# Cross-attention block with an MLP: gelus moved behind a copy, one normalization moved to VectorE, two batches' row loads moved into the fc pairs

## Chip, cores and metric

The kernel runs on one core of a Trainium2 chip. The metric is the device time of one execution in microseconds (us), lower is better; of several runs the median counts. The engines that matter here are TensorE (PE; PEld is its weight load), VectorE (DVE), ScalarE (ACT), GpSimd (POOL) and the queue of SyncE (SP), which issues most DMAs. Each engine works through its own list of instructions in order; semaphores tie the lists together.

## What is computed

Four batches (B = 4), 512 queries and 512 keys each, width 512, 16 heads of 32, inner width 2048, all in float32:

```python
residual = hidden
x = layer_norm(hidden, ln1_w, ln1_b)
q = (x @ q_w + q_b);  k = (ctx @ k_w + k_b);  v = (ctx @ v_w + v_b)      # split into heads
attn = softmax(where(mask, q k^T / sqrt(32), lowest))
hidden = (attn v) @ cproj_w + cproj_b + residual
y = layer_norm(hidden, ln2_w, ln2_b)
y = gelu(y @ fc_w + fc_b, approximate=True)
out = hidden + y @ proj_w + proj_b
```

## The kernel before

**Order.** Nothing is scheduled by a tool: the program order of each engine is the order in which the Python code emits instructions. The attention is emitted as 32 blocks (`block`), two for each of 16 groups `w` (a group is four heads of one batch; half a group is 256 queries). A table `fills` says for each block which other matmul work is put between its parts, to keep TensorE busy while VectorE and ScalarE work at the softmax: projections to q, k and v of later groups (`prep_q`, `prep_k`, `prep_v`), the output projection of a batch (`cproj`), transposes of normalized rows (`ln_turn`), and the MLP of batch 0 and half of batch 1. Each item has a cost (`CHAIN` = 3.4 for one accumulation chain, more for an fc pair); `run(work, budget)` emits items until the budget is used.

**A block.** `block` (L280) emits eight score tiles of [128, 512] (`scores`, L260), each into a PSUM bank of its own; there are eight banks, handed out in turn. `soften` adds the mask and takes the row minimum on VectorE (L266) and the exponential on ScalarE (L270). `turn` transposes 32x32 blocks on VectorE (L278). After the last exponential VectorE takes the reciprocal of the sums, and ScalarE spreads it (`rr`, L298, the "small copy"), VectorE transposes it (L301). `exchange` copies and DMAs the transposed weights between partitions, and a later `attend` multiplies them with v (L356) and divides (L361). ScalarE's tables hold either the exponential or the gelu: a switch is a table load in the trace.

**An fc pair.** The MLP's first matmul is done two f-chunks at a time by a Strassen-Winograd scheme of seven products (`fc_seven`, L487 on): product q1 goes to a bank, ScalarE copies it to `p1` (L518), and VectorE combines the other products with it in four additions (L471) that read the banks and write the pre-activation `g`. Then a gelu with the bias is due (L536), two activations for a pair. For pairs within the attention phase that gelu isn't emitted at once but put into a list, `S["gelu"]`, with the half `q` of the buffer that it works on; `gelus()` empties it. It is emptied in the next block directly behind the small copy `rr` (the call in `block`), inside `fc_seven` directly behind the copy to `p1`, and ahead of a projection that reads the half (`proj`, L571). In the pairs after the attention phase (`q is None`) the gelu is emitted directly.

**Normalization.** `ln_norm` (L143) computes (x - mean) * rstd for a tile of 128 rows, on ScalarE (L145) for the keys listed in `NORM_ACT`, otherwise on VectorE (L149). For `(2, 0)`, the second layer norm of batch 0, all four tiles are on ScalarE. `norm2(0, ...)` stands in the fill of block 10; the transposes to `yT` follow in the same block (L158), with their evictions on ScalarE (L163) and VectorE (L161).

**The last phase.** After the attention, `last_mlps` runs three MLPs: the other half of batch 1 (pairs 4 to 7), batch 2 and batch 3 (pairs 0 to 7 each). For each pair it emits weight sums for the next pair (`sum_wa`), the pair, the load of the weights of the pair after the next (`load_wa`, L595), in batch 1 also a load of projection weights (L814), and after every second pair the sums of two pairs' activations (`g_sums`, four operations on VectorE from SBUF to SBUF, L468 and L471). `project` then multiplies with the second weight matrix: a first product `q1p` (L716) that takes the last pair at the end, then `sums()`, then the other products (L698, or L661 where a second level of Strassen is used), the transposes of the next batch (`turns`), and the additions to the residual rows `hid` (`join`), whose results are stored.

**The residual rows.** The rows (attention result plus residual) of the later batches were written to a scratch tensor `xa` in HBM. `load_hid(b, ts)` reads them back by DMA on SP's queue (L412) and then adds the bias row `proj_b` on GpSimd (L367, one operation of [128, 512] for each of four tiles). In the trace the tile is `hl` for batch 2 and `hid` for the others. `sums()` in `last_mlps` calls it for the next batch, that is in the projection phase of the batch before:

```python
            def sums(b=b, new=new):
                for c in new[::2]:
                    p_sums(c)
                if b + 1 < B:
                    load_hid(b + 1, range(NT))
```

Of the kernel before, what the change touches and what calls it, by code (L numbers as in the profile page):

```python
# [21 lines left out]
B, L, D, H = 4, 512, 512, 16  # L22
HD = D // H
INNER = 4 * D
NT = L // P
# [8 lines left out]
SPLIT = 1  # L34
# [5 lines left out]
NORM_ACT = BY_ACT + ((2, 0), (2, 1))  # L40
# [10 lines left out]
def xattn_block(ctx: ExitStack, tc: tile.TileContext, x, encT, mask, q_w, k_w, v_w, c_w, fc_w, p_w, vecs, rows, out):  # L51
# [61 lines left out]
    S = {"gelu": []}  # L113
# [27 lines left out]
            S["nm", key] = nm  # L141

    def ln_norm(key, t, dst, src):  # L143
        if key in NORM_ACT:
            nc.scalar.activation(  # L145
                dst, src, AF.Identity, bias=S["nm", key][:, t : t + 1], scale=S["rs", key][:, t : t + 1]
            )
            return
        nc.vector.tensor_scalar(  # L149
            dst, src, S["mv", key][:, t, 0:1], S["rs", key][:, t : t + 1], ALU.subtract, ALU.mult  # L150
        )
# [103 lines left out]
    def scores(w, qt):  # L255
        qT, kT = S["qT", w], S["kT", w]
        S["sc", w, qt] = [acc_tile(f"sc_{w}_{qt}_{h}") for h in range(HG)]
        for h in range(HG):
            r = slice(h * HD, (h + 1) * HD)
            nc.tensor.matmul(S["sc", w, qt][h], qT[r, ts(qt, P)], kT[r, :], start=True, stop=True)  # L260

    def soften(w, qt, *heads):
        for h in heads:
            s = score_tile()
            mn = small.tile([P, 1], F32, tag="mn", bufs=2 * HG, name=f"mn_{w}_{qt}_{h}")
            nc.vector.tensor_tensor_reduce(  # L266
                out=s, in0=S["sc", w, qt][h], in1=S["mb", w // NG], scale=1.0, scalar=FMAX,
                op0=ALU.add, op1=ALU.min, accum_out=mn,
            )
            nc.scalar.activation(s, s, AF.Exp, bias=mn, scale=-1.0, accum_out=S["sums", w][:, qt, h : h + 1])  # L270
            if h % 2:
                S["ps", w, qt, h // 2] = score_pair()

    def turn(w, qt, k):

        tb = S["tb", w, qt // 2]
        tv = tb[:, :, :PW].rearrange("p j (a t h q) -> p a h t j q", a=2, t=NT, h=HG)
        nc.vector.transpose(tv[:, qt % 2, 2 * k : 2 * k + 2], S["ps", w, qt, k])  # L278

    def block(w, half, fill):  # L280

        q0, q1 = 2 * half, 2 * half + 1
        if half == 0:
            S["sums", w] = small.tile([P, NT, HG], F32, tag="sums", name=f"sums_{w}")
        tb = S["tb", w, half] = two.tile([P, NI, PW + 2 * HD], F32, tag="tb", name=f"tb_{w}_{half}")
        scores(w, q0)
        scores(w, q1)
        soften(w, q0, 0, 1, 2, 3)
        soften(w, q1, 0, 1)
        turn(w, q0, 0)  # L290
        turn(w, q0, 1)
        soften(w, q1, 2, 3)
        fill(0)
        turn(w, q1, 0)
        rs = small.tile([P, 2, HG], F32, tag="rsum", name=f"rsum_{w}_{half}")
        nc.vector.reciprocal(rs, S["sums", w][:, 2 * half : 2 * half + 2, :])
        rr = one.tile([P, 2, HG, HD], F32, tag="rr", name=f"rr_{w}_{half}")
        nc.scalar.copy(rr, rs[:, :, :, None].broadcast_to([P, 2, HG, HD]))  # L298
        gelus()
        turn(w, q1, 1)  # L300
        nc.vector.transpose(  # L301
            tb[:, :, PW:].rearrange("p j (a q) -> p a j q", a=2), rr.rearrange("p a h d -> p (a h d)")
        )
        waiting.append((w, half))
        last = w == NW - 1 and half
        if last:
            exchange()
        fill(1)
        if not last:
            exchange()  # L310
        fill(2)
# [7 lines left out]
    def exchange():  # L319

        while waiting and target(*waiting[0]) not in held:
            w, half = waiting.pop(0)
            held[target(w, half)] = w, half
            copies(w, half)
# [41 lines left out]
    def add_row(h, i):  # L366
        nc.gpsimd.tensor_tensor(h, h, row[:, i, :], ALU.add)  # L367
# [39 lines left out]
    def load_hid(b, ts_):  # L407

        for t in ts_:
            if ("hid", b, t) not in S:  # L410
                S["hid", b, t] = hids.tile([P, D], F32, tag="hid", name=f"hid_{b}_{t}")
            Q[0].dma_start(out=S["hid", b, t], in_=S["xa", b][ts(t, P), :])  # L412
        for t in ts_:
            add_row(S["hid", b, t], 1)

    def stat2(b, t):
        ln_stat((2, b), t, S["h", b, t])

    def norm2(b, t):
        h = S["h", b, t]  # L420
        y = tiles.tile([P, D], F32, tag="xn", name=f"xn2_{b}_{t}") if stays(b, t) else h
        S.setdefault(("yn", b), {})[t] = y
        ln_norm((2, b), t, y, h)
# [73 lines left out]
        return acc_tile(name).rearrange("p (i l) -> p i l", i=2)  # L497

    def gelus(q=None):
        while S["gelu"] and q in (None, S["gelu"][0][0]):  # L500
            S["gelu"].pop(0)[1]()

    def fc_seven(b, c, g, a, s, half, q=None):

# [34 lines left out]
        if q is None:  # L539
            gelus()  # L540
# [52 lines left out]
    def load_wa(c):  # L593
        for i in range(2):
            nc.sync.dma_start(out=wa[c % 2][:, i], in_=fc_w[:, 2 * c + i, :, :])  # L595

    def sum_wa(c):
        a = wa[c % 2]
        a_sums(a[:, 0, :2], a[:, 0, 2:], a[:, 1, :2], a[:, 1, 2:], *(ws[c % 2][:, i] for i in range(4)))
# [7 lines left out]
    def last_mlps():  # L607
# [71 lines left out]
        def g_sums(c):  # L679
            c = slice(c, c + 2)  # L680
            a11, a12, a21, a22 = (ga[:, c, k, j * HL : (j + 1) * HL] for j in range(2) for k in range(2))
            a_sums(a11, a12, a21, a22, gs[:, 0, c], gs[:, 1, c], a21, gs[:, 2, c])

        def fc_pair(b, c, sums):
            sums()
            fc_seven(b, c, ga[:, c], [wa[c % 2][:, i] for i in range(2)],
                     [ws[c % 2][:, i] for i in range(4)], half_tile)
# [97 lines left out]
        half = FIRST * FQ // 2  # L785
# [6 lines left out]
        def split(n):  # L792
            for _ in range(n):
                to_split.pop(0)()

        for b, pairs, new in (
            (SPLIT, range(half, NP), range(half)), (SPLIT + 1, range(NP), ()), (SPLIT + 2, range(NP), ())
        ):
            for c in pairs:

                def sums(b=b, c=c):
                    if c + 1 < NP:
                        sum_wa(c + 1)
                    split(splits.get((b, c), 0))

                fc_pair(b, c, sums)
                if c + 2 < NP:
                    load_wa(c + 2)
                elif b + 1 < B:
                    load_wa(c + 2 - NP)  # L810
                if new:
                    n = (c - half + 2) % half
                    for i in range(2):
                        nc.sync.dma_start(out=pb[:, n, i, :], in_=p_w[ts(2 * n + i, P), :])  # L814
                if c % 2 == 0 and c != pairs[0]:
                    g_sums(c - 2)

                if b == B - 3 and c < NP - 1:
                    stat2(B - 1, c - pairs[0])
                if b == B - 2:  # L820
                    if c == 0:
                        stat2(b + 1, NT - 1)
                        ln_rs((2, b + 1))
                    for t in {4: (0,), 5: (1, 2), 7: (3,)}.get(c, ()):
                        norm2(b + 1, t)
            g_sums(NP - 2)

            def sums(b=b, new=new):
                for c in new[::2]:
                    p_sums(c)  # L830
                if b + 1 < B:
                    load_hid(b + 1, range(NT))

            def turns(b=b):
                if b + 1 < B:
                    run(turns2(b + 1))
                if b == SPLIT:
                    load_xn(B - 1)

            def middle(b=b):  # L840
                if b + 1 < B:
                    y_sums(b + 1)
                    sum_wa(0)

            project(b, pairs, sums, turns, middle)
# [3 lines left out]
    CHAIN, TURN = 3.4, 0.5  # L849
# [115 lines left out]
    ahead, fills = {}, {}  # L965
# [20 lines left out]
    k, q, v = A(7)  # L986
    c, t2 = C(0), turns2(0)
# [4 lines left out]
    k, q, v = A(8)  # L992
    put(10, [k], norm(0, 0, 1), [v], norm(0, 2, 3), do(fc_sums), [q], t2, do(lambda: y_sums(0)))
    k, q, v = A(9)
# [4 lines left out]
    k, q, v = A(10)  # L999
# [4 lines left out]
    k, q, v = A(11)  # L1004
    put(16, h_(1, 0, 1), [k, q], x3[:2], some(2), x3[2:3])
    put(17, [v], x3[3:], h_(1, 2, 3), x4, cb(1), C(1))
    k, q, v = A(12)
    put(18, [q], some(2), [k])
    put(19, some(2), [v])
    k, q, v = A(13)  # L1010
    put(20, [k, q], stat(1, 0, 1, 2, 3), rs(1), some(2))
    put(21, [v], some(2))
    k, q, v = A(14)
# [3 lines left out]
    k, q, v = A(15)  # L1017
    c = C(2)
# [11 lines left out]
    for p in range(2 * NW):  # L1030
        w, half = divmod(p, 2)
        if half == 0 and w and w % NG == 0:
            make_mb(w // NG)
        run(ahead[p])
        for pair in due.get(p, ()):
            attend(*divmod(pair, 2))

        def fill(n, work=fills[p]):
            if n or not work or work[0][0] <= CHAIN:
                run(work, CHAIN if n < 2 else None)  # L1040

        block(w, half, fill)

    gelus()
    first_c = FIRST * FQ // 2
# [10 lines left out]
    c = C(B - 1)  # L1056
# [49 lines left out]
```

## Time and profile before

| | |
|---|---|
| median of three runs | 776.76 us (776.3 to 777.96) |
| the profiled execution's own time | 777.77 us |
| its span in the profile | 776.0 us |
| TensorE busy (matmul) | 770.2 us, 99% of the span |
| VectorE busy | 619.3 us, 80% |
| ScalarE busy | 337.3 us, 43% |
| GpSimd busy | 298.9 us, 39% |
| mean DMA rate | 154 GB/s |

How to read it: the span is what the hardware profiler saw of one execution; the rest of that execution's time, 1.77 us, lies around it. A matmul's end is modelled, so a matmul that stands a little longer in the record than its kind usually does has in most cases waited. In a timeline, the text in brackets at the end of a row is how long the engine was idle ahead of the instruction and what ended the wait. "x8" groups neighbouring instructions of one kind; a group's time runs from the first start to the last end, so a wait inside a group shows as a longer group. PEclk is the clock that TensorE was granted, 1.00 being full.

### The profile page before, as it was taken

The numbers are of one execution on the slowest core, as the hardware profiler recorded it, in microseconds if no ns is written. First come the engines' busy times: TensorE is split into PE (matmuls) and PEld (weight loads), VectorE is DVE, ScalarE is ACT, GpSimd is POOL, SyncE is SP. The second block draws the span as 40 slices with busy tenths as digits, with TensorE's granted clock in tenths as the row PEclk, the third lists the DMA queues.
The fourth block names the chain that finished last, engine by engine and source line by source line (L and its number), as shares of the span: only waits on it lengthen the run. The fifth ranks groups of instructions, "written<-read, shape, count | busy, mean of one in ns | idle before, by whom it ended". The sixth has DMA issues, their size and how long they took to land.

```text
span 776.0 us, 12991 instructions
## 1 busy us (share of the span) xinstructions
PE 770.2 (99%) x4450; PEld 522.3 (67%) x4450; DVE 619.3 (80%) x1262; ACT 337.3 (43%) x761; POOL 298.9 (39%) x311
## 2 busy tenths in 40 slices
PE   9999999999999999999999999999999999999998
PEld 7656455566654745565554566446888889988897
DVE  3889899886888757887888988856878999669863
ACT  2676766574675445737753467501201221012200
POOL 1525446378353264233575444430060024300052
PEclk9999999999999999999999999999999999999999
DMA  8978779456755666665657866683623330023001
GB/s 326 322 224 226 180 197 274 108 149 167 204 146 155 181 183 168 162 177 130 162 127 193 215 195 194 151 256 122 196 92 92 95 110 14 29 82 95 1 16 41
DMA packets 54817, 119.37 MB, mean 154 GB/s; under 512 B 10416, under 2 KB 13616, under 8 KB 54624
## 3 DMA queue, kind: packets, MB, share of 16 engines
q1 hardware_dynamic: 53712, 115.71, 53.5%
q0 software_dynamic: 896, 2.82, 1.2%
q8 instruction: 35, 0.57, 0.3%
q14 instruction: 30, 0.25, 0.1%
q10 hardware_dynamic: 144, 0.02, 0.0%
HBM read 58.22 MB, written 6.82 MB: 84 GB/s over the span
## 4 chain that ended last, share of the span: by engine, by line
PE 93%; DVE 4%; ACT 1%; issue 1%; POOL 0%; DVEq 0%; POOLq 0%
PE q L515 24%; PE accp L571 11%; PE sc L260 9%; PE av L356 7%; PE r L661 7%; PE accc L396 7%; PE accv L240 7%; PE acck L217 7%; PE accq L229 7%; PE q4p L698 2%; PE tp L158 2%; PE q1p L716 1%; DVE ptt L266 1%; DVE ga L471 1%; DVE gs L468 1%; PE warm L898 1%
## 5 line engine op out<-in xcount | busy, mean ns | idle before, releaser
L270 ACT ACTIVATE ptt<-ptt,mn 128x512 f32<-128x512 f32 x256 | 181.6, 711 | 157.2 <-DVE mn L266 157.2
L266 DVE CUSTOM_DVE_ANT_0 ptt<-sc,mb 128x512 f32<-128x512 f32 x256 | 160.5, 682 | 17.3 <-PE sc L260 17.3
L278 DVE STREAM_TRANSPOSE tb<-ptt 128x1024 f32<-128x1024 f32 x128 | 153.5, 1218 | 0.3 <-ACT ptt L270 0.2
L334 POOL COPY pT<-tb 32x1088 f32<-32x1088 f32 x96 | 104.3, 1086 | 42.6 <-DVE oT L361 20.9
L571 PE MATMUL accp<-pbt,gt 128*128 128x512 f32 x192 | 86.6, 606 | 0.0
L515 PE MATMUL q<-yT,gt 128*128 128x256 f32 x320 | 78.9, 379 | 0.0
L260 PE MATMUL sc<-pbt 32*128 32x512 f32 x512 | 71.3, 616 | 0.2 <-DVE gt L471 0.2
L571 PEld LDWEIGHTS accp<-pbt,gt 128*128 128x128 f32 x192 | 36.4, 193 | 47.0 <-issue 40.6
L536 ACT ACTIVATE ga<-ga,vec 128x512 f32<-128x512 f32 x40 | 26.7, 715 | 94.9 <-DVE ga L471 94.9
L515 PEld LDWEIGHTS q<-yT,gt 128*128 128x128 f32 x320 | 60.9, 190 | 8.6 <-issue 0.5
L240 PEld LDWEIGHTS accv<-ptt,xe 128*128 128x128 f32 x512 | 59.1, 192 | 7.4 <-DVE mn L266 4.7
L515 PE MATMUL q<-ys,gt 128*128 128x256 f32 x240 | 61.7, 380 | 0.0
L240 PE MATMUL accv<-ptt,xe 128*128 128x128 f32 x512 | 60.0, 276 | 0.0
L217 PE MATMUL acck<-xe,ptt 128*128 128x512 f32 x128 | 58.8, 602 | 0.0
L229 PE MATMUL accq<-xe,ptt 128*128 128x512 f32 (+1 forms) x136 | 58.3, 573 | 0.0
L396 PE MATMUL accc<-wc,oT 128*128 128x512 f32 x128 | 56.4, 596 | 0.0
L515 PEld LDWEIGHTS q<-ys,gt 128*128 128x128 f32 x240 | 45.6, 190 | 6.5 <-DVE gt L468 0.4
L260 PEld LDWEIGHTS sc<-pbt 32*128 32x128 f32 x512 | 29.2, 184 | 29.3 <-issue 17.5
L270 ACT ACTIVATION_READ_ACCUMULATOR ptt<-ptt,mn 128x1 f32 x256 | 47.9, 187 | 0.0
L356 PE MATMUL av<-pT,v 128*32 128x256 f32 x768 | 46.4, 382 | 0.0
L252 POOL TENSOR_TENSOR v<-v,row 128x512 f32<-128x512 f32 x16 | 20.3, 1269 | 67.8 <-ACT v L245 67.3
L229 PEld LDWEIGHTS accq<-xe,ptt 128*128 128x128 f32 x136 | 25.0, 190 | 30.8 <-issue 23.2
(181 smaller groups left out, 1187.8 us busy)
## 6 DMA issues: line engine op xcount, KB each, us to landing
pT<-tb SPq DMA_DIRECT2D x288, 136.0 KB, 2.4
pbt<-p_w_dram SPq DMA_DIRECT2D x40, 256.0 KB, 3.0
gt<-fc_w_dram SPq DMA_DIRECT2D x40, 256.0 KB, 2.6
gt<-tb SPq DMA_DIRECT2D x48, 136.0 KB, 2.4
xe<-tb SPq DMA_DIRECT2D x48, 136.0 KB, 2.4
pbt<-fc_w_dram SPq DMA_DIRECT2D x24, 256.0 KB, 4.2
ptt<-k_w_dram SPq DMA_DIRECT2D x16, 256.0 KB, 3.4
xe<-encT_dram SPq DMA_DIRECT2D x16, 256.0 KB, 5.0
```

Source lines behind the costliest of these rows:

```text
L217: nc.tensor.matmul(acc, S["wk", w][:, d, :], eT[:, d, :], start=(d == 0), stop=(d == ND - 1))
L229: nc.tensor.matmul(acc, S["wq", w][:, d, :], xT[:, d, c], start=(d == 0), stop=(d == ND - 1))
L240: nc.tensor.matmul(acc[:, ts(t, P)], eT[:, d, ts(t, P)], S["wv", w][:, d, :], start=(d == 0), stop=(d == ND - 1),)
L260: nc.tensor.matmul(S["sc", w, qt][h], qT[r, ts(qt, P)], kT[r, :], start=True, stop=True)
L266: nc.vector.tensor_tensor_reduce(out=s, in0=S["sc", w, qt][h], in1=S["mb", w // NG], scale=1.0, scalar=FMAX, op0=ALU.add, op1=ALU.min, acc ...
L270: nc.scalar.activation(s, s, AF.Exp, bias=mn, scale=-1.0, accum_out=S["sums", w][:, qt, h : h + 1])
L278: nc.vector.transpose(tv[:, qt % 2, 2 * k : 2 * k + 2], S["ps", w, qt, k])
L334: nc.gpsimd.tensor_copy(pT[ts(i, HD), i], tb[ts(i, HD), i])
L356: nc.tensor.matmul(av[ts(h, HD), : 2 * P].rearrange(shape, **kw), v[:, t, ts(h, HD)], p[t][h], start=(t == 0), stop=(t == NT - 1),)
L396: nc.tensor.matmul(acc, S["oT", b][:, g, ts(t, P)], wc[:, g, :], start=(g == 0), stop=(g == NG - 1))
L515: nc.tensor.matmul(o, x[:, k], y[:, k], start=(k == 0), stop=(k == 1))
L571: nc.tensor.matmul(acc, gT[q % 2][:, k, ts(t, P)], S["pw", b, q * FQ + k], start=(k == 0), stop=(k == FQ - 1))
```

## The change

Four edits:

- `block` gets a flag `pairs`, true if the block's fill has an item dearer than `CHAIN`, which only an fc pair is. Where it is true, `gelus()` isn't called behind the small copy; the waiting gelus are then emitted by the next fc pair's own call, behind its copy to `p1`. The order changes in five blocks: ahead of pairs 1, 2, 3 and 7 of batch 0 and pair 3 of batch 1, the table load and two gelus of the pair before, which stood ahead of the copy to `p1`, stand behind it.
- `gelus(q)` takes all waiting items of half `q` wherever they stand in the list, instead of stopping at the first of another half. The order of instructions doesn't change by this.
- `ln_norm` puts tile 3 of `(2, 0)` on VectorE. That instruction now follows the transpose of `rr` on VectorE (L301) and precedes the evictions to `yT`.
- `load_hid` isn't called in `sums()` any more, but inside the loop over pairs: for batch 2 after pair 5 of batch 1, for batch 3 after pair 3 of batch 3 itself. Four DMA issues on SP and four additions on GpSimd move each time.

TensorE's list is the same instruction for instruction.

```diff
     def ln_norm(key, t, dst, src):
-        if key in NORM_ACT:
+        if key in NORM_ACT and (key, t) != ((2, 0), 3):
...
-    def block(w, half, fill):
+    def block(w, half, fill, pairs):
...
         nc.scalar.copy(rr, rs[:, :, :, None].broadcast_to([P, 2, HG, HD]))
-        gelus()
+        if not pairs:
+            gelus()
         turn(w, q1, 1)
...
     def gelus(q=None):
-        while S["gelu"] and q in (None, S["gelu"][0][0]):
-            S["gelu"].pop(0)[1]()
+        for item in list(S["gelu"]):
+            if q in (None, item[0]):
+                S["gelu"].remove(item)
+                item[1]()
...
                 if c % 2 == 0 and c != pairs[0]:
                     g_sums(c - 2)
 
+                if (b, c) in ((SPLIT, half + 1), (B - 1, half - 1)):
+                    load_hid(max(b, SPLIT + 1), range(NT))
                 if b == B - 3 and c < NP - 1:
                     stat2(B - 1, c - pairs[0])
...
             def sums(b=b, new=new):
                 for c in new[::2]:
                     p_sums(c)
-                if b + 1 < B:
-                    load_hid(b + 1, range(NT))
...
-        block(w, half, fill)
+        block(w, half, fill, any(cost > CHAIN for cost, _ in fills[p]))
```

Here `SPLIT` is 1, `B` is 4 and `half` is 4.

## The prediction

> **What bounds the kernel now.** I read the page first: its span, then the chain that ended last.
>
> ```profile
> span 776.0 us, 12991 instructions
> PE 93%; DVE 4%; ACT 1%; issue 1%; POOL 0%; DVEq 0%; POOLq 0%
> ```
>
> TensorE is on the chain for 93% of the span, and the change removes no matmul. What can be won is time in which its matmuls stand further apart than usual. The chain in order of time (start, length) shows where: equal batches of matmuls with unequal lengths.
>
> ```profile
> 180.88 1.93 PE sc L260 x16
> 194.34 3.85 PE sc L260 x16
> 226.78 3.85 PE sc L260 x16
> 230.63 15.63 PE accp L571 x32
> 367.63 2.66 PE sc L260 x16
> 502.11 13.93 PE accp L571 x32
> ```
>
> The eight scores of a block take 1.93 us undisturbed; three batches take 3.85, 3.85 and 2.66. One batch of projections takes 15.63 instead of 13.93. The timeline around the first long batch of scores tells why.
>
> ```profile
> 191.03 1.28 ACT L536 ACT_TABLE_LOAD   x1
> 192.33 1.33 ACT L536 ACTIVATE gt<-gt,vec 128x512 f32<-128x512 f32 x2
> 193.57 0.35 ACT L518 COPY p<-q 128x256 f32<-128x256 f32 x1
> 193.94 1.28 ACT L270 ACT_TABLE_LOAD   x1
> 193.95 0.69 DVE L471 TENSOR_TENSOR gt<-q,p 128x512 f32<-128x512 f32 x1 [2.07 <-ACT p L518]
> 196.75 0.62 PEld L260 LDWEIGHTS sc<-pbt 32*128 32x128 f32 x4 [0.44 <-DVE gt L471]
> 197.67 0.72 ACT L270 ACTIVATE ptt<-ptt,mn 128x512 f32<-128x512 f32 x1 [2.45 <-DVE mn L266]
> ```
>
> ScalarE loads the gelu table and runs two gelus of the previous pair; only then does it copy p1 of this pair. VectorE stands idle 2.07 us for that copy, its additions empty the pair's PSUM banks late, and the scores, which need those banks, wait for `gt`.
>
> **Part 1, the gelus.** In five blocks (pairs 1, 2, 3 and 7 of batch 0, pair 3 of batch 1) the table load and the gelus now stand behind p1, so p1 can start up to 1.28 + 1.33 = 2.6 us earlier and the additions when VectorE is free. At 194 and at 226 the scores should return to 1.93: 2 x 1.92. At 367 the gain is 2.66 - 1.93 = 0.73. The pair of batch 1 shows in the timeline:
>
> ```profile
> 485.40 1.37 PE L260 MATMUL sc<-pbt 32*128 32x512 f32 x8
> 489.68 2.84 PE L571 MATMUL accp<-pbt,gt 128*128 128x512 f32 x6
> ```
>
> Scores from 485.40 to the next work at 489.68 are 4.28 us, less 1.93 = 2.35. The fifth block (pair 2) has a value projection behind its pair and no long batch of scores: nothing. Sum 1.92 + 1.92 + 0.73 + 2.35 = 6.92. What the gelus now stand ahead of on ScalarE are the table load for the exponentials and the exponentials. It is the same work in another order, so the load still ends at 193.94 + 1.28 = 195.22; the first exponential would be due at 197.67 - 1.92 = 195.75, 0.5 us later. The gelus' readers, the projections, come a block or more afterwards. Bounds: 3.5 (half of it) to 6.92; I take 6.92, as the block at 180.88, with a pair ahead but no waiting gelu, shows no stall.
>
> The long batch of projections is a consequence, in this execution. In the view by windows (TensorE's busy time, count, granted clock, DMA share, GB/s), the first stall and what follows the second:
>
> ```profile
> 194.20:198.20 4.00, 4.00 (x21) 1.00 0.83 294
> 230.50:234.50 4.00, 4.00 (x7) 0.57 0.77 176
> ```
>
> Right behind the second stall the clock is 0.57 for 4 us, worth 15.63 - 13.93 = 1.70 us. Without the stall I expect no such fall: 1.70 of the profiled execution; bounds 0 to 1.70.
>
> By the Trainium skill ("TensorE: Matmul & The Clock Gate", Part 1) the clock halves after an idle window of about 3.4 us whose phase runs free. That would fit one fall after two equal stalls, though neither stall was idle throughout; and it speaks against the change in Part 4, where a new stall near that length may appear.
>
> **Part 2, one norm on VectorE.** Norm 3 of batch 0 leaves ScalarE.
>
> ```profile
> 158.61 1.52 ACT L145 ACTIVATE xn<-h,nm,rs 128x512 f32<-128x512 f32 x2
> 160.18 1.64 PE L158 MATMUL tp<-ident,xn 128*128 128x128 f32 x13 [0.38 <-ACT xn L145]
> 160.99 1.53 DVE L161 TENSOR_SCALAR yT<-tp,vec 128x512 f32<-128x512 f32 x2 [2.29 <-PE tp L158]
> 633.56 0.54 DVE L149 TENSOR_SCALAR hn<-hn,mv,rs 128x512 f32<-128x512 f32 x1
> ```
>
> VectorE is idle for 2.29 us ahead of 160.99, from 158.7, and the like instruction takes 0.54: done at 159.25. ScalarE's remaining norm 2 ends at 158.61 + 0.76 = 159.4, and the transpose that waited until 160.18 can go at about 159.6. Gain 0.6. Bounds: 0 (if GpSimd holds VectorE up) to 0.8 (a whole norm).
>
> **Part 3, batch 3's rows leave the projections of batch 2.**
>
> ```profile
> 635.60 6.30 POOL L367 TENSOR_TENSOR hid<-hid,row 128x512 f32<-128x512 f32 x4 [44.20 <-DMA hid<-xa]
> 635.77 1.64 DVE L468 TENSOR_TENSOR ga<-ga 128x512 f32<-128x512 f32 x1
> 643.09 0.68 DVE L468 TENSOR_TENSOR pbt<-pbt 128x512 f32<-128x512 f32 x1
> 646.29 1.52 DVE L161 TENSOR_SCALAR yT<-tp,vec 128x512 f32<-128x512 f32 x2
> 647.15 2.05 PE L661 MATMUL r<-pbt,gs 128*128 128x128 f32 x16 [0.61 <-DVE yT L161]
> ```
>
> While GpSimd adds four rows, VectorE's sums from SBUF to SBUF take 1.64 instead of 0.68. Four such make it some 4 us late; it empties the transposes' banks only from 646.29, and TensorE waits 0.61. Without them that wait should go: gain 0.6, bounds 0 to 1.0 (the transposes ahead may close up a little too).
>
> By the Trainium skill ("SBUF — State Buffer", "SBUF: two separate sides") a VectorE operation with two SBUF inputs and a GpSimd operation that reads SBUF exclude each other for whole instructions. By it the cost does not vanish but goes with the rows to wherever VectorE does such sums. The row of 1.64 agrees; Part 4 is the case.
>
> **Part 4, batch 2's rows move into the pairs of batch 1.** The rows of before, the new neighbours first (pairs 6 and 7 of batch 1), then the old place, then a longer first projection for the length of one matmul:
>
> ```profile
> 544.33 0.90 SPq L814 DMA_DIRECT2D pbt<-p_w_dram  x2
> 550.80 0.68 DVE L471 TENSOR_TENSOR gs<-ga 128x512 f32<-128x512 f32 x1
> 554.27 0.67 DVE L471 TENSOR_TENSOR ga<-q,p 128x512 f32<-128x512 f32 x1
> 557.03 1.33 ACT L536 ACTIVATE ga<-ga,vec 128x512 f32<-128x512 f32 x2 [4.52 <-DVE ga L471]
> 555.85 3.62 PE L716 MATMUL q1p<-pbt,ga 128*128 128x256 f32 x16
> 557.50 1.75 SPq L412 DMA_DIRECT2D hl<-xa  x4
> 562.42 6.82 POOL L367 TENSOR_TENSOR hl<-hl,row 128x512 f32<-128x512 f32 x4 [43.58 <-DMA hl<-xa]
> 562.99 1.77 DVE L468 TENSOR_TENSOR ptt<-pbt,ptt 128x512 f32<-128x512 f32 x1
> 569.71 0.68 DVE L468 TENSOR_TENSOR ptt<-pbt,ptt 128x512 f32<-128x512 f32 x1
> 727.52 7.07 PE L716 MATMUL q1p<-pbt,ga 128*128 128x256 f32 x32
> ```
>
> The four DMA issues, 1.75 us of SP's queue, now follow the p_w loads at 544.33, from 545.23. Behind them in that queue stand only the next batch's first weights: nothing. The first addition came 562.42 - 557.50 = 4.92 us after the first issue; so the additions now run from about 550.15 to 557.0. From 550.80 VectorE makes the four sums of pairs 4 and 5. Four sums beside such additions took 569.71 - 562.99 = 6.72 us, against 4 x 0.68 = 2.7 alone: 4.0 us late. Queued behind them on VectorE are the additions of the last pair (554.27), and on these wait its gelus (557.03; the first done at 557.70). The first projection takes that pair last: 12 of its 16 matmuls at (7.07 - 3.62) / 16 = 0.216 us come first, until 555.85 + 2.59 = 558.44. The gelu has 0.74 us to spare; 4.0 - 0.74 = 3.3 us of standstill, or 3.0 as the last sum outlasts GpSimd. Bounds: 0 (rows landing some 3 us later, behind the sums) to 3.3, and 1.7 more if the clock falls again. A gain is excluded, since the sums from 562.99 on held up no matmul. I take 3.0: the row of 4.92 has the same queue and the same neighbours ahead.
>
> Batch 3's rows now come during its own pairs, beside these sums:
>
> ```profile
> 710.61 0.68 DVE L471 TENSOR_TENSOR gs<-ga 128x512 f32<-128x512 f32 x1
> 728.45 1.33 ACT L536 ACTIVATE ga<-ga,vec 128x512 f32<-128x512 f32 x2 [4.40 <-DVE ga L471]
> ```
>
> About two sums are stretched, 2 us. The last pair's first gelu, done at 729.1, is needed at 727.52 + 28 x 0.216 = 733.57: slack 4.4, cost 0, bounds 0 to 0.5.
>
> **The sum.** The profiled execution took 777.77 (776.0 span and 1.77 around it): 777.77 - 6.92 - 1.70 - 0.6 - 0.6 + 3.0 = 770.95. The median of the three timed runs is 776.76, 1.0 lower; if these had no fall of the clock, 776.76 - 6.92 - 0.6 - 0.6 + 3.0 = 771.6. I forecast 771.2.
>
> **Rivals.** (a) Batch 2's rows hide: they land behind the four sums. Then 771.2 - 3.0 = 768.2. For: landing hangs on what else the DMA queue moves; against: the row of 4.92. (b) The new stall drops the clock as at 230.5: 771.2 + 1.7 = 772.9. For: it is longer than the stall that did it; against: the equal stall at 194 did not. (c) The gelus' move does half: the scores' last banks wait next for what stands behind the additions on VectorE (the `oT` product, the `h` addition): 771.2 + 3.5 = 774.7. Against: the block at 180.88. It is also the case in which the change does not do what it says. (d) Slower: both batches' additions hold VectorE up until TensorE stands still, 3.3 us in each and each with a fall of the clock: 2 x 5.0 = 10.0 against 6.92 + 0.6 + 0.6 = 8.1 at the median: 776.76 + 1.9 = 778.6. It decides from the point where batch 3's delay exceeds its 4.4 us of slack. For: the same kind of sums stand in both batches' pairs; against: only two of batch 3's meet the additions.
>
> **How the numbers follow.** Forecast 0.45, (a) 0.20, (b) 0.15, (c) 0.11, (d) 0.09. A measurement here tells 0.2%, 1.6 us, from no change. The first four lie below 775.2 but for a tail of (c), 0.05: faster 0.86, same 0.05, slower 0.09. The range takes (a) with some spread below, and (c): 767.6 to 775.0; outside lie (d) and the tails.
>
> **What would show it.** Right: scores of 1.93 at all four places, p1 ahead of the gelus' table load, no granted clock under 1 near 230; batch 0's transposes without the wait for ScalarE; `r` behind the transposes of batch 2 without one for VectorE; `hl` additions beside four sums of about 1.7, and q1p of batch 1 in two pieces, 3 us apart. Wrong: scores still near 3.8, q1p unbroken (then 768), or exponentials that wait for a table load.

## The result, and the profile after

| | before | changed |
|---|---|---|
| median of 14 runs each, same chip | 776.36 us (775.48 to 780.8) | 771.6 us (771.11 to 775.7) |
| span of the profiled execution | 776.0 us | 769.8 us |
| ratio of the medians | | 0.9941, interval 0.9926 to 0.9955 |

The change makes the kernel faster by 0.6%. The forecast was 771.2.

All lines of code below the edits stand a few lines later in the changed kernel: the copy to `p1` is L521, the additions of a pair and all such sums L469 and L472, the gelus L539, the projections L574, the addition of rows L368, `r` L664, `q1p` L719. First the span and the chain's shares by engine, from the page of the changed kernel:

```profile
span 769.8 us, 12991 instructions
...
PE 97%; DVE 2%; DMA 0%; issue 0%; ACT 0%; POOL 0%; DVEq 0%; POOLq 0%
```

TensorE has gone from 93% to 97% of the chain: less of the span is spent in waits for others. Then the chain of the changed kernel in order of time (start, length, what), at the places that the prediction named:

```profile
163.34 2.55 PE sc L260 x16
...
194.47 1.93 PE sc L260 x16
...
224.98 1.93 PE sc L260 x16
226.91 13.93 PE accp L574 x32
...
362.21 1.93 PE sc L260 x16
...
479.31 2.23 PE sc L260 x16
...
552.97 1.13 PE q1p L719 x4
...
641.18 25.09 PE r L664 x224
```

Three batches of scores that took 3.85, 3.85 and 2.66 us take 1.93, the projections at 226.91 are back from 15.63 to 13.93, and the one in the pair of batch 1 takes 2.23. Two rows speak the other way: scores at 163.34 (2.08 before) and the four last matmuls of `q1p`, which now stand by themselves.

The same chain, cut into stages at work that both kernels have, says where the time went. Each stage is the difference of two start times in that view:

| stage, from and to | before | changed | difference |
|---|---|---|---|
| transposes at 143 to the projections at 230 | 143.07 to 230.63 | 143.32 to 226.91 | -3.97 |
| to the next matmuls `accc` x32 | to 272.47 | to 267.05 | -1.70 |
| to the projections `accp` x32 at 502 | to 502.11 | to 493.91 | -2.78 |
| from `accc` at 518 to the first `q4p` of batch 1 | 517.90 to 578.70 | 509.70 to 573.33 | +2.83 |
| to the first `q4p` of batch 2 | to 672.43 | to 666.27 | -0.79 |
| to the last `q4p` | to 765.86 | to 759.70 | 0.00 |

They add up to -6.41. The start up to 143 is 0.25 later in this execution, and -6.41 + 0.25 = -6.16 is the difference of the spans, 6.2.

The timeline of the changed kernel around the first cured batch of scores shows how:

```profile
191.05 0.36 ACT L521 COPY p<-q 128x256 f32<-128x256 f32 x1
191.43 1.28 ACT L539 ACT_TABLE_LOAD   x1
...
191.93 0.66 DVE L472 TENSOR_TENSOR gt<-q,p 128x512 f32<-128x512 f32 x1
...
192.72 1.33 ACT L539 ACTIVATE gt<-gt,vec 128x512 f32<-128x512 f32 x2
194.07 1.28 ACT L270 ACT_TABLE_LOAD   x1
194.40 2.00 PE L260 MATMUL sc<-pbt 32*128 32x512 f32 x16
```

The copy now ends at 191.41 and VectorE's additions start at 191.93, as soon as VectorE is through with its transpose; before, they stood behind table load, gelus and copy. The gelus run beside the additions. The table for the exponentials is there at 194.07 + 1.28 = 195.35, and the first exponential starts at 196.29 because its maximum comes then: the gelus' new place costs nothing, as forecast.

The new wait stands in the timeline of the changed kernel between the last pairs of batch 1:

```profile
541.86 6.29 POOL L368 TENSOR_TENSOR hl<-hl,row 128x512 f32<-128x512 f32 x4 [30.95 <-PE q L518]
...
542.55 1.13 DVE L472 TENSOR_TENSOR gs<-ga 128x512 f32<-128x512 f32 x1
...
543.71 1.64 DVE L469 TENSOR_TENSOR ga<-ga 128x512 f32<-128x512 f32 x1
...
545.28 1.75 DVE L469 TENSOR_TENSOR gs<-gs,ga 128x512 f32<-128x512 f32 x1
...
547.06 1.64 DVE L469 TENSOR_TENSOR gs<-ga,gs 128x512 f32<-128x512 f32 x1
...
547.64 2.75 PE L719 MATMUL q1p<-pbt,ga 128*128 128x256 f32 x12
...
549.44 0.67 DVE L472 TENSOR_TENSOR ga<-q,p 128x512 f32<-128x512 f32 x1
...
552.20 1.33 ACT L539 ACTIVATE ga<-ga,vec 128x512 f32<-128x512 f32 x2 [7.94 <-DVE ga L472]
552.97 1.13 PE L719 MATMUL q1p<-pbt,ga 128*128 128x256 f32 x4 [2.58 <-ACT ga L539]
```

Read from the top: GpSimd adds the four rows from 541.86 to 548.15. The first addition starts 4.66 us after the first issue of the rows' DMAs at 537.20, where 4.92 was forecast. (The bracket names a matmul and not the transfer as what ended the wait; in the version with batch 2's rows alone, below, the same wait ends with the transfer.) Four sums on VectorE fall into that time and take 1.13 to 1.75 us instead of 0.68. The additions of the last pair, queued behind them, start at 549.44; its gelus start at 552.20; and TensorE, which has done 12 of 16 matmuls, stands still for 2.58 us.

The rest of part 3, at the end of batch 2, is in the timeline of the changed kernel too:

```profile
640.13 1.53 DVE L161 TENSOR_SCALAR yT<-tp,vec 128x512 f32<-128x512 f32 x2 [3.17 <-PE tp L158]
641.02 2.03 PE L664 MATMUL r<-pbt,gs 128*128 128x128 f32 x16
```

VectorE is idle for 3.17 us ahead of the evictions, where it was late before, and `r` no longer has a wait of 0.61 in brackets.

### The profile page after: what moved, and what is told of

It is laid out like the page before. It is cut to its first block, busy times and chain, and to the rows that moved or that the text cites. A ratio compares the mean times of both kernels' runs of the same rounds, so it can differ in the third digit from the quotient of the medians.

```text
span 769.8 us, 12991 instructions
## 1 busy us (share of the span) xinstructions
PE 762.7 (99%) x4450; PEld 519.1 (67%) x4450; DVE 616.4 (80%) x1263; ACT 336.8 (44%) x760; POOL 298.1 (39%) x311
## 4 chain that ended last, share of the span: by engine, by line
PE 97%; DVE 2%; DMA 0%; issue 0%; ACT 0%; POOL 0%; DVEq 0%; POOLq 0%
PE q L518 24%; PE accp L574 11%; PE sc L260 8%; PE av L357 8%; PE accv L240 8%; PE acck L217 7%; PE accq L229 7%; PE r L664 7%; PE accc L397 7%; PE q4p L701 2%; PE q1p L719 2%; PE tp L158 2%; PE q2p L701 1%; DVE ga L472 1%; PE warm L901 1%; PE q3p L701 0%
## 5 line engine op out<-in xcount | busy, mean ns | idle before, releaser
L574 PE MATMUL accp<-pbt,gt 128*128 128x512 f32 x192 | 84.9, 596 | 0.0
L539 ACT ACTIVATE ga<-ga,vec 128x512 f32<-128x512 f32 x40 | 26.7, 714 | 98.5 <-DVE ga L472 98.5
L574 PEld LDWEIGHTS accp<-pbt,gt 128*128 128x128 f32 x192 | 35.8, 190 | 45.9 <-issue 39.4
L260 PE MATMUL sc<-pbt 32*128 32x512 f32 x512 | 65.3, 614 | 0.0
L397 PEld LDWEIGHTS accc<-wc,oT 128*128 128x128 f32 x128 | 23.8, 190 | 30.8 <-issue 27.4
```

What stands on the lines that cost most here:

```text
L397: nc.tensor.matmul(acc, S["oT", b][:, g, ts(t, P)], wc[:, g, :], start=(g == 0), stop=(g == NG - 1))
L574: nc.tensor.matmul(acc, gT[q % 2][:, k, ts(t, P)], S["pw", b, q * FQ + k], start=(k == 0), stop=(k == FQ - 1))
```

## The experiments

Each version was timed together with the kernel before on the same chip, and the time that it is set against below is the median of that kernel there. "Stage" is a stage of the table above, measured in the profiled execution.

### Each part on the kernel before

**The gelus alone.** The kernel before with the edits of `block` and `gelus` only.

```diff
-    def block(w, half, fill):
+    def block(w, half, fill, pairs):
...
-        gelus()
+        if not pairs:
+            gelus()
...
-        while S["gelu"] and q in (None, S["gelu"][0][0]):
-            S["gelu"].pop(0)[1]()
+        for item in list(S["gelu"]):
+            if q in (None, item[0]):
+                S["gelu"].remove(item)
+                item[1]()
```

> The kernel before with the gelus' edit alone. Theory: p1 ahead of the gelus gives back the stretched scores, 3.85, 3.85, 2.66 and 4.28 us to 1.93, 1.93, 1.93 and 2.23 as in the changed kernel: 6.6 us, so about 769.8 against 776.4, and no granted clock under 1 near 225 us. Rival: the gelus are only part of it and the other edits carry the gain: 774 or more. Rival: the stall goes into the exponentials: scores short, but ScalarE waits for a table load and the projections' av behind it.

Measured: 770.11 us (769.89 to 770.88) against 777.58, ratio 0.9907 (0.9888 to 0.9925). The first stage is 83.70, 3.86 less than before, without the norm's edit. The ratio is lower than that of the whole change, though by the intervals only just (up to 0.9925 here, from 0.9926 there). The stages say the same more clearly: that of batch 1 is 60.79 (571.70 - 510.91) where the changed kernel has 63.63, and what the changed kernel has ahead is 0.11 in the first stage and 0.90 in that of batch 2 (93.84 against 92.94). So the other parts of the change cost time in sum.

**The norm alone.**

```diff
-        if key in NORM_ACT:
+        if key in NORM_ACT and (key, t) != ((2, 0), 3):
```

> The kernel before with the norm alone on VectorE. Prediction's step: 0.6 us gained, 775.8. Theory from the changed kernel's trace: the transposes gain 0.35, but VectorE's next sum then meets GpSimd's weight sums (1.16 instead of 0.68), the scores wait longer (2.55 instead of 2.08 us) and 0.1 to 0.2 is left: 776.2, no difference that can be measured. Again a look at the clock behind the stall at 227 us.

Measured: 776.71 us (775.9 to 779.74) against 777.58, ratio 1.0001 (0.9987 to 1.0014); the first stage 87.44 against 87.56. Nothing that the medians can tell, 0.12 us in the stage.

**Batch 3's rows alone.**

```diff
+                if (b, c) == (B - 1, half - 1):
+                    load_hid(B - 1, range(NT))
...
-                if b + 1 < B:
+                if b == SPLIT:
                     load_hid(b + 1, range(NT))
```

> The kernel before with batch 3's rows alone moved into its pair 3. Theory: the sums in the projections of batch 2 fall from 1.64 to 0.69, the wait of 0.61 behind the transposes is gone and 0.8 is gained, nothing is lost in batch 3's pairs: 775.6. Rival: the additions stretch sums in batch 3's pairs until TensorE waits there: 776.4 or more.

Measured: 775.61 us (775.22 to 778.01) against 777.48, ratio 0.9981 (0.9966 to 0.9996). The chain in order of time of this kernel, from the first `q4p` of batch 1 to that of batch 2:

```profile
577.34 3.45 PE q4p L698 x16
...
670.29 6.91 PE q4p L698 x32
```

670.29 - 577.34 = 92.95, against 93.73 before: 0.78, the same as in the changed kernel. The stage behind it is as long as before, so the rows cost nothing in their new place.

**Batch 2's rows alone.**

```diff
+                if (b, c) == (SPLIT, half + 1):
+                    load_hid(SPLIT + 1, range(NT))
...
-                if b + 1 < B:
+                if SPLIT < b < B - 1:
                     load_hid(b + 1, range(NT))
```

> The kernel before with batch 2's rows alone moved into pair 5 of batch 1. Theory: four sums of about 1.7 us beside GpSimd's additions, the first projection of batch 1 in two pieces with 2.6 us between, and 776.4 + 2.6 = 779.0. Rival: no wait, 776.4. The gelus' stalls are still in it, so its profile shows a further time whether the clock falls behind the stall at 227 us (1.7 us) or not.

Measured: 781.91 us (778.33 to 784.97) against 777.58, ratio 1.0052 (1.003 to 1.0075): slower, as the only part. The waits of TensorE in this kernel:

```profile
PE q1p L716 <- ACT ga L536: 3.2, 1, 3.2
```

That is one wait of 3.2 us. The stage is 65.90 against 60.80, 5.10 longer, more than the wait. The view by windows has the rest (PE, PEld, DVE, ACT, POOL busy with counts, then the granted clock, DMA share, GB/s):

```profile
232.00:236.00 4.00, 4.00 (x7) 1.55 (x6) 4.00 (x10) 3.48 (x10) 3.88 (x4) 0.57 0.83 193
560.00:564.00 4.00, 1.19 (x4) 0.98 (x5) 2.40 (x4) 1.33 (x2) 0.00 (x0) 0.90 0.46 131
564.00:568.00 4.00, 4.00 (x14) 3.31 (x13) 3.90 (x7) 0.58 (x1) 0.00 (x0) 0.67 0.00 0
```

The clock is down to 0.57 behind the scores' stall at 228, as in the kernel before, and to 0.67 behind the new stall. There the four matmuls behind the wait take 1.75 us instead of 0.86, and the rest of the 5.10, about 1 us, is lost in the matmuls that follow. The expectation of 779.0 had the wait without this. All nine executions have a mean clock below 1.0 (0.993 to 0.999); behind which stall the others lost it isn't known, as only one was profiled.

### What in the moved rows costs the time

**Batch 2's rows back in the projections.** The changed kernel, with this one move undone.

```diff
-                if (b, c) in ((SPLIT, half + 1), (B - 1, half - 1)):
-                    load_hid(max(b, SPLIT + 1), range(NT))
+                if (b, c) == (B - 1, half - 1):
+                    load_hid(B - 1, range(NT))
...
+                if b == SPLIT:
+                    load_hid(b + 1, range(NT))
```

> The changed kernel, with batch 2's rows loaded where they were before (projections of batch 1) and batch 3's rows at their new place. Theory: the 2.58 us wait of the first projection of batch 1 goes and nothing comes in its place, since the rows' additions then meet sums that held up no matmul: 771.6 - 2.6 = 769.0, faster than the changed kernel. Rival: the wait is due to something else in the changed order, or the old place costs the same elsewhere: 771.6.

Measured: 768.85 us (768.19 to 769.3) against 777.58, ratio 0.989 (0.9871 to 0.9909). The stage is 60.79, as before the change. The move costs 63.63 - 60.79 = 2.84 us.

**The transfers without the additions.** The changed kernel with the DMAs of batch 2's rows at their new place, and without GpSimd's four additions to them, so that the output of batch 2 lacks the bias row.

```diff
             for t in ts_:
-                add_row(...)
+                if b != SPLIT + 1:
+                    add_row(...)
```

> The changed kernel, leaving out the four additions of the bias row to batch 2's rows (the output of batch 2 lacks proj_b); the DMAs stay at the new place. Theory: the additions on GpSimd stretch the sums, so without them the sums take 0.69, the wait of the first projection of batch 1 is gone, 769.0. Rival: the DMAs (their traffic, or SP's queue) cause the wait: it stays at 2.6, 771.6.

Measured: 768.65 us (768.12 to 769.52) against 777.48, ratio 0.9883 (0.9862 to 0.9904). The chain of this kernel (its lines from L413 on stand one later):

```profile
510.47 13.93 PE accc L397 x32
...
548.57 3.46 PE q1p L720 x16
...
571.26 3.45 PE q4p L702 x16
```

`q1p` is in one piece again and the stage 571.26 - 510.47 = 60.79. The transfers and their issues cost nothing; the whole price is GpSimd's four additions. VectorE's sums take 0.68 to 0.69 here, so it isn't their place or their data that makes them long.

**One pair earlier.** The changed kernel with batch 2's rows after pair 4 of batch 1.

```diff
-                if (b, c) in ((SPLIT, half + 1), (B - 1, half - 1)):
+                if (b, c) in ((SPLIT, half), (B - 1, half - 1)):
```

> The changed kernel with batch 2's rows loaded after pair 4 of batch 1 instead of pair 5. Theory (only sums with two SBUF operands are stretched, and only by GpSimd's additions): the additions run some 6 us earlier and meet the weight sums for pair 7 (four of 256 elements, 0.41 each alone) instead of the four sums of 512; these become 1 us longer each or less, VectorE can make up a part, and the wait shrinks to between 0 and 2 us: 769.0 to 771. Rival: VectorE has no time to spare in these pairs, so the wait stays at 2.6 whichever sums are met: 771.6.

Measured: 770.96 us (769.77 to 773.36) against 777.48, ratio 0.9916 (0.9892 to 0.994); the stage 62.42, 1.62 more than before. The timeline of this kernel:

```profile
536.53 5.14 POOL L368 TENSOR_TENSOR hl<-hl,row 128x512 f32<-128x512 f32 x4 [25.31 <-DMA hl<-xa]
...
539.83 0.72 DVE L472 TENSOR_TENSOR gt<-gt 128x256 f32<-128x256 f32 x1 [1.78 <-DMA gt<-fc_w_dram]
540.47 2.28 DVE L469 TENSOR_TENSOR gt<-gt 128x256 f32<-128x256 f32 x3
...
552.33 1.13 PE L719 MATMUL q1p<-pbt,ga 128*128 128x256 f32 x4 [1.36 <-ACT ga L539]
```

Here GpSimd's additions meet the sums of weights `gt` instead of the sums of activations; three of these take 2.28 instead of the 1.21 of the kernel before. They also start later, as the weights land later: VectorE waits 1.78 for them, against 1.03 before. Together this delays the last pair, and the wait is 1.36. So the price hangs on what the additions meet. That the transfers, free at the place after pair 5, delay the weights at this one is read from the order; no run has them here without the additions.

**Batch 3's rows two pairs later.** Batch 2's rows back, batch 3's after pair 5 of batch 3, where they meet the pairs as batch 2's do in the change.

```diff
-                if (b, c) == (B - 1, half - 1):
+                if (b, c) == (B - 1, half + 1):
                     load_hid(B - 1, range(NT))
```

> The version with batch 2's rows back at their old place, with batch 3's rows loaded after pair 5 of batch 3 instead of pair 3. Theory: the additions now stretch all four sums of pairs 4 and 5, some 4 us late; the last pair's gelu has 4.4 us to spare before the first projection needs it, so q1p stays unbroken (6.91 us from its start to the next), but the sums ahead of the second level of products come late by up to 4 us and may cost 0 to 1.5 us there: 768.9 to 770.4. Rival: the slack was misread, q1p of batch 3 breaks in two as that of batch 1 did, by 2 us or more: 771.

Measured: 768.84 us (768.47 to 769.63) against 778.71, ratio 0.9882 (0.9854 to 0.991). The timeline of this kernel:

```profile
710.02 2.16 DVE L469 TENSOR_TENSOR gt<-gt 128x256 f32<-128x256 f32 x3
710.44 5.32 POOL L368 TENSOR_TENSOR hid<-hid,row 128x512 f32<-128x512 f32 x4 [49.27 <-DMA hid<-xa]
...
712.88 1.95 DVE L472 TENSOR_TENSOR ga<-q,ga 128x512 f32<-128x512 f32 x3
...
714.74 1.57 DVE L472 TENSOR_TENSOR gs<-ga 128x512 f32<-128x512 f32 x1
```

The last stage stays at 93.43. The rows landed earlier than I had assumed, and met the weight sums and one of the four activation sums rather than all four. The pair's own additions at 712.88, which read a bank `q` beside SBUF, lie wholly within GpSimd's work and still take 1.95 for three: only sums with both inputs in SBUF are stretched. As one activation sum is stretched here, this doesn't test whether batch 3's slack would have covered four stretched sums; that part of the question stays open.

### What became of the norm

**The weight sums behind the y sums.** In the first stage of the changed kernel the wait ahead of the transposes is gone, and yet only 0.1 us is won. Its timeline:

```profile
159.33 2.15 PE L158 MATMUL tp<-ident,xn 128*128 128x128 f32 x16
...
161.97 0.73 POOL L469 TENSOR_TENSOR wsum<-wsum,pbt 128x256 f32<-128x256 f32 x1
162.09 1.16 DVE L469 TENSOR_TENSOR ys<-yT 128x512 f32<-128x512 f32 x1
...
163.28 2.62 PE L260 MATMUL sc<-pbt 32*128 32x512 f32 x16
...
164.31 0.41 DVE L362 TENSOR_TENSOR oT<-av,pT 128x256 f32<-128x256 f32 x1
```

VectorE's first sum of `y` falls onto GpSimd's sums of weights (`wsum`) and takes 1.16; `oT`, behind it in VectorE's queue, frees the banks that the scores need, and the scores take 2.62. The kernel before has the same two sums side by side:

```profile
162.40 1.30 POOL L468 TENSOR_TENSOR wsum<-pbt,wsum 128x256 f32<-128x256 f32 x1
162.44 0.68 DVE L468 TENSOR_TENSOR ys<-yT 128x512 f32<-128x512 f32 x1
...
163.62 2.15 PE L260 MATMUL sc<-pbt 32*128 32x512 f32 x16
```

There GpSimd's sum is the one that is stretched (1.30 instead of 0.73), and VectorE's is not. It isn't always so: in the profile with batch 2's rows alone, where this part of the program is that of the kernel before, GpSimd's sum takes 0.73 and VectorE's 1.23, and the scores take 2.69 even with the norm on ScalarE. So the collision was there already; which engine pays for it differs between profiles of the same program, and what decides that isn't shown.

If the collision is what takes the gain, the norm should be worth its 0.6 as soon as these weight sums (`fc_sums`) stand behind the y sums. Tried on the version with batch 2's rows back:

```diff
-    put(10, [k], norm(0, 0, 1), [v], norm(0, 2, 3), do(fc_sums), [q], t2, do(lambda: y_sums(0)))
+    put(10, [k], norm(0, 0, 1), [v], norm(0, 2, 3), [q], t2, do(lambda: y_sums(0)), do(fc_sums))
```

> Batch 2's rows back at their old place, and the first weight sums on GpSimd (block 10) emitted behind the transposes and the y sums of that block instead of ahead. Theory: VectorE's two y sums no longer meet GpSimd's weight sums, take 0.68 instead of 1.16 and 1.03, and the scores behind them return to 1.93 from 2.55: 0.6 us under the version with the rows back alone, 768.4; the weight sums end some 2 us before the first pair needs them. Rival: the weight sums come too late for the first pair, which then waits: 769.5 or more.

Measured: 768.58 us (767.94 to 769.99) against 777.48, ratio 0.9884 (0.9862 to 0.9905), span 766.3. The timeline of this kernel:

```profile
161.98 0.68 DVE L469 TENSOR_TENSOR ys<-yT 128x512 f32<-128x512 f32 x1
...
163.16 2.00 PE L260 MATMUL sc<-pbt 32*128 32x512 f32 x16
163.38 0.42 DVE L362 TENSOR_TENSOR oT<-av,pT 128x256 f32<-128x256 f32 x1
```

The sums take 0.68, `oT` comes at 163.38 and the scores take 2.00.

**The same with the norm back on ScalarE**, to tell the norm's share from that of the weight sums.

```diff
-        if key in NORM_ACT and (key, t) != ((2, 0), 3):
+        if key in NORM_ACT:
```

> The fastest version so far (batch 2's rows back, first weight sums later) with norm 3 of batch 0 back on ScalarE. Theory: the norm's gain was there but was taken back by the collision of the y sums with GpSimd; with the collision gone it counts, so without the norm the way from the transposes at 143 us to the 32 projections at 226 us is 82.97 + 0.4 = 83.4 us or a little more. Rival: the norm is worth nothing in any surroundings: 82.97.

Measured: 768.77 us (768.14 to 770.08) against 778.71, ratio 0.9877 (0.9844 to 0.991). The medians don't tell these two apart. The first stage does, with the gelus moved in all four:

| first stage, us | weight sums ahead | weight sums behind |
|---|---|---|
| norm 3 on ScalarE | 83.70 | 83.56 |
| norm 3 on VectorE | 83.59 | 82.97 |

By these, each edit alone is worth 0.11 and 0.14, both together 0.73, and the norm is worth 0.59 where nothing collides behind it. Each cell is one profiled execution. Five versions have this stage as in the lower left cell, and they give 83.59 to 83.85; the two long ones wait some 0.2 more at the `av` matmuls near 193, far behind the norm. So 0.59 and 0.73 are clear of that spread, and 0.11 and 0.14 aren't.

A shorter stretch shows the 0.11 as well. From the transposes at 143 to the matmuls `acck` behind the scores it takes 22.57 to 22.59 in six profiles with the norm on VectorE, and 22.69 to 22.70 in three with it on ScalarE; in the fourth of these, the one in which VectorE's sum was stretched, it takes 23.24.

The best version here is the one with the gelus and the norm as in the change, batch 3's rows as in the change, batch 2's rows in the projections and the weight sums behind the y sums: 768.58 us. That the weight sums' move helps the median by itself (768.85 without it) isn't shown, only the 0.63 in the profiled stage.

## Why the prediction was right, and where it was off

**The gelus: right, 6.62 of 6.92.** 1.92 + 1.92 + 0.73 came as worked out. In the pair of batch 1 it was 2.05 instead of 2.35: the scores take 2.23, not the 1.93 that the prediction took for granted there. In the timeline of the changed kernel VectorE's additions there end only after the scores should start:

```profile
477.50 1.95 DVE L472 TENSOR_TENSOR gt<-q,gt 128x512 f32<-128x512 f32 x3
...
479.24 2.30 PE L260 MATMUL sc<-pbt 32*128 32x512 f32 x16
479.36 0.68 DVE L578 TENSOR_TENSOR h<-accp,h 128x512 f32<-128x512 f32 x1
479.95 0.41 DVE L362 TENSOR_TENSOR oT<-av,xe 128x256 f32<-128x256 f32 x1
```

Behind them stand the `h` addition and `oT`, which rival (c) had named as the next wait; here it takes 0.30, not half of the gain. That this is what holds the scores is read from the order, not tried.

**The clock: right in the profiled execution, a matter of chance over many.** The 15.63 became 13.93 and 1.70 was won in the span. But the fall behind the old stalls doesn't come every time: the profiled executions with the norm alone and with batch 3's rows alone have both long batches of scores (3.85 and 3.86) and projections of 13.93 behind them, while in the one with batch 2's rows alone the clock fell behind the second of these stalls and behind its new one. So making the sum twice, with the fall and without, was needed. Without the 1.70 the stages give -6.41 + 1.70 = -4.71, and the medians differ by 771.6 - 776.36 = -4.76.

**The norm: the term that was mis-sized, 0.6 forecast and about 0.1 measured.** The step that failed is that a gain at the transposes is passed on. The transposes did lose their wait of 0.38, and the `av` matmuls behind them start 0.59 earlier after the transposes at 143 (18.16 instead of 18.75), so the 0.6 itself was right; then the scores take 2.55 instead of 2.08, as VectorE's sums of `y` are held up by GpSimd's weight sums. I had GpSimd in the lower bound, at the norm itself; it struck one step later. The four versions of the table above show it.

**Batch 3's rows leaving: right, 0.79 for 0.6.** The wait of 0.61 is gone, and the 224 matmuls of `r` take 25.09 instead of 25.28, another 0.19 that I had only in the bound. Alone it measures 0.78.

**Batch 2's rows: right, 2.83 for 3.0, and for the reason given.** Additions from 541.86, four sums of up to 1.75, the last pair's additions and gelus late, TensorE idle for 2.58. Undoing the move gives it back, leaving out the additions alone gives it back, and one pair earlier, where it meets other sums, it is 1.62. Rival (a), that the rows hide, falls. One size was off: the four sums make the last pair 3.42 us late, not 4.0, since the first of them meets the additions only in part (1.13). The remainder of the 2.83 lies in the four matmuls behind the stall, 1.13 instead of 4 x 0.216 = 0.86.

**Batch 3's rows in their own pairs: right, 0.** The last stage is the same to 0.01 us, so rival (d) falls. The collision is there, and the slack takes it: in the changed kernel three weight sums take 2.16 instead of 1.21 and one sum of activations 1.65 instead of 0.69, together the 2 us of the forecast, though it had put them on two sums of activations.

**Rival (b), a fall of the clock behind the new stall: not in the median.** The profiled execution of the change shows none, that with batch 2's rows alone does (0.67). Of the 14 executions three have a mean granted clock of 0.996 to 0.998 and take 773.2, 773.64 and 775.7; the median is at a clock of 1.0. That these three lost it behind the new stall isn't shown, as they weren't profiled. The six versions that have neither the scores' stalls nor this one stay between 767.9 and 770.9, with clocks of 0.999 and 1.0.

The sum thus came out close because two misses partly cancel: the gelus and the norm brought 0.3 and 0.5 less than forecast, the rows cost 0.17 less and gave 0.19 more. Together this leaves the gain 0.44 smaller than the sum had it. That the sum without a fall of the clock, 771.6, hits the measured median to the digit is luck: it starts from 776.76, the median of three runs, and over 14 runs that median came out 0.40 lower.

## What to carry to other kernels

A scheduling edit is priced where its engine next meets another: two of four parts here ran into a collision of VectorE's SBUF-to-SBUF sums with GpSimd, which cost one of them its gain and made the other a loss. Before moving work to GpSimd's idle time, list which of VectorE's operations with both inputs in SBUF run then, and who waits behind them. And a bundle of edits is worth taking apart even if it wins: one edit alone gained at least as much as the four together, and without the one bad move the kernel takes 768.85 instead of 771.6.

## What the runs showed of the hardware

- VectorE sums of [128, 512] float32 with both inputs in SBUF take 0.68 us alone and 1.64 to 1.75 beside GpSimd's additions; those with one input in PSUM keep their 0.65 (1.95 for three) beside the same work. I had the first from the trace of before, not the second. GpSimd can be the one stretched instead: its sum of [128, 256] took 1.30 instead of 0.73 beside a VectorE sum of 0.68.
- The granted clock falls to 0.57 or 0.67 over the next 4 us behind a stall of some 2 to 3 us in some executions and not in others, with the same instructions. Batch 3's rows alone shows it in its single times: seven of 12 executions at 775.22 to 775.63 with a clock of 1.0, five at 776.99 to 778.01 with 0.997 to 0.998. What decides it wasn't found.
- The start of the kernel, up to the transposes at 143, ended between 143.07 and 145.19 in the profiled executions of versions that don't differ there. That is more than some of the effects studied, so stages were compared rather than spans.
